# Linear attention in chunks: the product of queries and running states, as one product on 128 rows or as two on 64

## The chip, the cores and the metric

The kernel runs on one core of a Trainium2 chip. The core has five engines that work at the same time, each from its own queue in order: TensorE (PE, matrix products; its weight loads are shown as PEld), VectorE (DVE), ScalarE (ACT), GpSimd (POOL) and SyncE (SP), which here only starts transfers. The metric is the time on the device in microseconds (us), the median of several runs.

## The reference

Two transformer layers over 16 sequences (batches) of 512 tokens with 128 channels, all in float32. Each layer is: norm, scale and shift; an attention; a gated residual; norm, scale and shift; a feed-forward part; a gated residual.

In layer 0 the attention is causal and linear, with 16 heads of 8 channels. In layer 1 it is a retention with a decay per head, which has the same form once the decay is folded into q and k:

```python
# layer 0, for each token t and head:
S = S + kt[..., :, None] * vt[..., None, :]
z = z + kt
num = jnp.einsum('bhi,bhij->bhj', qt, S)
den = jnp.sum(qt * z, axis=-1, keepdims=True)
y = num / (den + EPS)
# layer 1:
retention = jnp.einsum('bhsd,bhtd->bhst', q, k) * SCALING * decay   # decay is 0 above the diagonal
out = jnp.einsum('bhst,bhtd->bhsd', retention, v)                    # then a norm per head and a gate
```

Layer 0's feed-forward part is a channel mix with a token shift. Layer 1's is an attention over the 16 batches at the same time step, followed by a choice of one of eight experts per token. This last part is called the routed half below.

## The kernel before

**Two halves.** The causal half runs both attentions and the channel mix, batch by batch (`both_layers`), and stores rows to DRAM (`token_rows`). The routed half reads them back by time step and runs the attention over batches and the experts. The change is in the causal half only.

**How a batch is laid out.** Channels lie on the 128 partitions (rows), tokens along the free dimension. The 16 heads are in four groups `r` of four (`RG`, `RH`); group `r` has the rows 32r to 32r+31 of q and k. The 512 tokens are 16 chunks of 32 (`NCH`, `CH`), in four blocks `g` of 128 tokens with four chunks `c` each; chunk number is `4 * g + c`. Each head has nine value columns, eight values and a one for the denominator (`HV`), so a group has 36 columns.

**The attention over chunks, `attended` (L659).** It has two parts that are planned side by side, and a third after both.

- `states_before`: the keys are turned (L672). PE forms, for each chunk, the products of keys and values (L685, tiles of 64 rows by 32 columns, 72 columns long). DVE masks away products of different heads (L699) and sums over chunks (a scan, L707). ACT and POOL each copy two of the four 32-row groups into `state` (L722). `state` is zero elsewhere, so it is a block diagonal: for each chunk 128 rows by 4 x 36 columns.
- `within_chunks`: ACT writes `kh`, the keys with one head each (L651). PE multiplies queries and keys inside each chunk on tiles of 32 rows by 32 columns (L752), two head groups at a time. ACT copies the scores (L761), PE turns them (L767), DVE applies the causal mask (L734). PE multiplies them with the values into two PSUM banks `o_ps` (L785), as tiles of 128 rows by 32 columns, 36 columns long.
- Last, PE adds queries times the state before the chunk (L801): one product per chunk from all 128 rows, 144 columns long, on a tile of 128 by 32. Bank `a` holds the blocks `g = 2a` and `2a + 1`. The first chunk has no state before it, so 15 products remain, in two bursts `n`.

Layer 0 divides the sums by the denominator (DVE, L870 to L872). Layer 1 takes a norm per head: ACT squares (L976), DVE sums (L978), ACT takes a root (L980), DVE divides (L982, L983). The result `y` is then turned and projected (L818, L602).

**The order of the work.** Each engine's order is written out by hand. Every chain of steps is a Python generator that yields marks such as `"P1.2"` (next comes a step on PE, planned at 1.2 us). `queued` keeps up to `WIDTH` = 5 batches running, always takes the step that can start first by its planned times, and emits its instructions; so the planned times and starts decide the order in every queue, including SP's, whose transfers wait in order as well. Batch n+1 may begin `SPACE` us of planned time after batch n, or when one of the five is done if that is later. Earlier batches have priority up to batch 12.

Of the kernel before, what the change touches and what calls it, by code (L numbers as in the profile page):

```python
# [22 lines left out]
F32 = mybir.dt.float32  # L23
# [6 lines left out]
P = 128  # L30
# [14 lines left out]
WIDTH = 5  # L45
CALM = 4.0
RUN, RUN_US = 5, 8.5
SPACE, SPACE2 = 10.0, 5.0
NX = WIDTH + 1
LATE = 12  # L50
LANDING = 4.5
# [161 lines left out]
def tile_adaln(ctx: ExitStack, tc: tile.TileContext, x, wa, wb, vec, wex, const, out):  # L213
# [122 lines left out]
    def groups(t):  # L336
        return t.rearrange("p (g m) -> p g m", m=P)
# [258 lines left out]
    def at_chunk(ch):  # L596
        return ch % NG * NC + ch // NG
# [61 lines left out]
    def attended(b, own_values, q, k):  # L659
# [57 lines left out]
        def copied(n, sums):  # L717
            yield "G1.5" if n else "A1.4"
            for r in range(n, RG, 2):
                rows = slice(r * 32, (r + 1) * 32)  # L720
                copy = nc.gpsimd.tensor_copy if n else nc.scalar.copy
                copy(state[rows, r], sums[rows])  # L722

        def within_chunks():
            yield "A2.7"

            kh = masked(own_set, k)
            by_block = q.rearrange("p (n s) -> p n s", s=CH)
            past = []

            def causal_only(rr, st_ps):
                yield "V1.3"
                for r, t in enumerate(st_ps):
                    tt(  # L734
                        sc[:, 2 * rr + r].rearrange("p (n t) -> p n t", t=CH),
                        t.rearrange("p (n t) -> p n t", t=CH),
                        causal.unsqueeze(1).to_broadcast([P, NCH, CH]),
                        ALU.mult,
                    )
                back(*st_ps)  # L740
                yield ""
                past.append(rr)

            for rr in range(2):
                s_ps = yield from banks(2)
                yield "P1.4"
                for n in range(NG):
                    for c in range(NC):
                        for r in range(2):
                            rows = slice((2 * rr + r) * 32, (2 * rr + r + 1) * 32)  # L750
                            at = at_chunk(n * NC + c)
                            mm(  # L752
                                groups(s_ps[r])[c * CH : (c + 1) * CH, n],
                                lhsT=by_block[rows, at],
                                rhs=kh[rows, at].rearrange("p m s -> p (m s)"),
                                start=True,
                                stop=True,
                            )
                yield "A1.2"
                for r in range(2):  # L760
                    nc.scalar.copy(sc[:, 2 * rr + r], s_ps[r])  # L761
                back(*s_ps)
                st_ps = yield from banks(2)
                yield "P1.25"
                for r in range(2):
                    for n in range(NG):
                        nc.tensor.transpose(  # L767
                            groups(st_ps[r])[:, n], groups(sc[:, 2 * rr + r])[:, n], ident
                        )
                yield Begun([causal_only(rr, st_ps)])  # L770

            yield ""
            while not past:
                yield "D0.1"
            yield from landed_at(("heads", own_values))
            o_ps.extend((yield from banks(2)))
            for r in range(RG):
                while len(past) <= r // 2:
                    yield "D0.1"
                yield "P0.45"  # L780
                for n in range(2):
                    for c, a in turns:
                        g = 2 * a + n
                        k0 = (n * RG + r) * RH * HV
                        mm(  # L785
                            o_ps[a][c * CH : (c + 1) * CH, k0 : k0 + RH * HV],
                            lhsT=groups(sc[:, r])[:, g, c * CH : (c + 1) * CH],
                            rhs=vh[:, g * NC + c, :, r * HV : (r + 1) * HV],
                            start=n == 0 and r == 0,
                            stop=False,  # L790
                            skip_group_check=True,
                        )

        turns = [(c, (c + d) % 2) for d in range(2) for c in range(NC)]
        yield [states_before(), within_chunks()]
        for n in range(2):
            yield "P1.2"
            for c, a in turns:
                ch = (2 * a + n) * NC + c
                if ch:  # L800
                    mm(  # L801
                        o_ps[a][c * CH : (c + 1) * CH, n * NH * HV : (n + 1) * NH * HV],
                        lhsT=q.rearrange("p (n s) -> p n s", s=CH)[:, at_chunk(ch)],
                        rhs=state[:, :, :, ch - 1].rearrange("p r j -> p (r j)"),
                        start=False,
                        stop=n == 1,
                        skip_group_check=True,
                    )
        free_values.append(own_values)
        free_sets.append(own_set)  # L810
        return o_ps, [o[:, 0 : 2 * NH * HV].rearrange("p (n k) -> p n k", k=HV) for o in o_ps]

    def closed(b, y, w, finish):

# [20 lines left out]
    def linear_attention(b):  # L835
        w = own(b, [P, NGATE, C], "gated")
        yield Begun([closing_weights(b, w)] + [next_entry(b + 1)] * (WIDTH <= b < B - 1))
        yield from landed_at(("x", b))
        h = work("h", b)
        yield from norm(b, mod0, 0, h, spread)  # L840
        own_values = yield from taken(free_values)
        qk = [work(tag, b) for tag in "qk"]

        def queries_and_keys():
            qk_ps = yield from banks(2)
            yield "P1.9"
            for a in range(2):
                mm(qk_ps[a], lhsT=wa_col(A_ATTN + a * C), rhs=h, start=True, stop=True)

            yield [positive(a, qk_ps[a]) for a in range(2)]  # L850

        def positive(a, ps):
            yield "A1.3"
            t = qk[a]
            nc.scalar.activation(t, ps, AF.Relu, scale=-1.0)
            nc.scalar.activation(t, t, AF.Exp, scale=-1.0)
            yield "V0.7"
            stt(t, ps, 0.0, t, ALU.max, ALU.add)  # L858
            back(ps)

        yield [
            queries_and_keys(),
            spread_values(b, h, wa_col(A_ATTN + 2 * C), own_values),
        ]
        o_ps, halves = yield from attended(b, own_values, *qk)
        y = work("q", b)
        for a, o in enumerate(halves):
            yield "V1.0"
            rd = own(b, [P, 2 * NH], "rd", bufs=2)
            ts(rd, o[:, :, HD], DEN_EPS, None, ALU.add)  # L870
            nc.vector.reciprocal(rd, rd)
            tt(  # L872
                y[:, a * 2 * C : (a + 1) * 2 * C].rearrange("p (n d) -> p n d", d=HD),
                o[:, :, 0:HD],
                rd.unsqueeze(2).to_broadcast([P, 2 * NH, HD]),
                ALU.mult,
            )
            back(o_ps[a])

        def finish(yt, y_ps):  # L880
            yield "A0.6"
            nc.scalar.copy(yt, y_ps)
            back(y_ps)

        yield from closed(b, y, w[:, 0], finish)
        return w
# [36 lines left out]
    def retention(b, w):  # L923
# [47 lines left out]

        def head_norm(a, o):
            yield "A0.4"
            yv = y[:, a * 2 * C : (a + 1) * 2 * C].rearrange("p (n d) -> p n d", d=HD)
            rd = own(b, [P, 2 * NH], "rd", bufs=2)
            nc.scalar.activation(yv, o[:, :, 0:HD], AF.Square)  # L976
# [6 lines left out]
            tt(yv, o[:, :, 0:HD], rd.unsqueeze(2).to_broadcast([P, 2 * NH, HD]), ALU.mult)  # L983
            back(o_ps[a])

        yield [head_norm(a, o) for a, o in enumerate(halves)]
# [830 lines left out]
```

## Time and profile before

| What | Value |
|---|---|
| Median of 3 runs | 1081.94 us (1080.48 to 1090.74) |
| The profiled execution | 1088.3 us, its span 1086.5 us |
| Mean granted TensorE clock | 0.923 |
| L801 in the causal half | 960 matmul instructions, 78.1 us busy |
| First and last of L801 | 56.4 and 700.6 us |
| Fetch of x by batch, from the sixth on (us) | 167.7, 195.8, 213.3, 251.4, 309.3, 376.0, 401.6, 430.3, 465.6, 519.1 |
| Last store of a residual (`token_rows<-k`) | 712.2 us |

A row of the profile names the line, the engine, the operation, the tile written and those read, their shapes, and how often. "128*32" ahead of a matmul's shape is the part of the 128 by 128 array that it uses. A float32 product appears as two matmul instructions. Busy time of a group is the union of its instructions, which on PE overlap. "Idle before" is the time in which the engine stood still just before instructions of the group, with what released them. The chain that ended last is followed back from the last instruction.

### The profile page before, as it was taken

Reading aid. Unit: us, or ns where it says so; the run is one execution under the profiler, and the core shown is the slowest. Engines: PE = TensorE matmul, PEld = TensorE weight load, DVE = VectorE, ACT = ScalarE, POOL = GpSimd, SP = SyncE. Lnnn points to the kernel's source line nnn. Section 1 sums busy time; section 2 is a strip of 40 time slices with the busy share of each in tenths; the row PEclk is TensorE's granted clock in tenths of the full one; section 3 lists DMA queues with packets and bytes.
Section 4 is the critical chain, followed back from the end, with each engine's and each line's share of the span. In section 5 each row is a group of like instructions: output and inputs, shape, how many; then the busy total and the mean of one; then the engine's idle time right before and its main releaser. Section 6 shows DMA issues by size and latency. Waiting matters only on the chain.

```text
span 1086.5 us, 37454 instructions
## 1 busy us (share of the span) xinstructions
PE 899.0 (83%) x15423; PEld 644.8 (59%) x15423; DVE 800.9 (74%) x2404; ACT 633.4 (58%) x1196; POOL 499.3 (46%) x621
## 2 busy tenths in 40 slices
PE   5798989896999898998889988738679777866985
PEld 4565666655666666665556665525456556755864
DVE  8567788885787889887688687647878767856444
ACT  3465554764645567574536555419878757744654
POOL 3313344542343453434343262234672565775676
PEclk9799999998899999999988998869788889998998
DMA  5624522524133333333232304050156364558763
GB/s 182 148 63 95 140 45 60 130 52 97 46 68 68 77 81 80 77 77 70 59 61 53 68 22 87 24 173 2 65 175 219 121 233 144 163 171 277 237 197 99
DMA packets 147851, 116.92 MB, mean 108 GB/s; under 512 B 75061, under 2 KB 127544, under 8 KB 147552
## 3 DMA queue, kind: packets, MB, share of 16 engines
q1 hardware_dynamic: 141024, 96.57, 33.9%
q0 software_dynamic: 6368, 17.08, 4.2%
q8 instruction: 122, 2.00, 0.7%
q10 hardware_dynamic: 288, 0.86, 0.3%
q14 instruction: 49, 0.40, 0.1%
HBM read 66.46 MB, written 39.04 MB: 97 GB/s over the span
## 4 chain that ended last, share of the span: by engine, by line
PE 41%; DVE 25%; ACT 10%; issue 8%; POOL 7%; DMA 6%; SPq 2%; POOLq 0%; another core or an unknown queue 0%; DVEq 0%; ACTq 0%
PE bank L602 6%; PE bank L801 4%; DVE q L550 4%; PE bank L752 3%; PE bank L767 3%; PE bank L1614 3%; PE bank L785 2%; PE bank L939 2%; PE bank L685 2%; DVE sc L734 2%; PE bank L940 2%; POOL out_x L1690 2%; DVE added L707 2%; DVE st L514 2%; DMA v_chunks<-values 2%
## 5 line engine op out<-in xcount | busy, mean ns | idle before, releaser
L761 ACT COPY sc<-bank 128x512 f32<-128x512 f32 x128 | 68.5, 588 | 78.9 <-PE bank L752 78.2
L550 DVE TENSOR_SCALAR q<-x,mv,rs 128x128 f32<-128x128 f32 x240 | 85.8, 421 | 21.6 <-POOL rs L523 13.9
L722 POOL COPY states<-added 32x576 f32<-32x576 f32 x64 | 43.5, 679 | 116.8 <-DVE added L707 91.2
L734 DVE TENSOR_TENSOR sc<-bank,con 128x512 f32<-128x512 f32 x128 | 81.8, 678 | 17.9 <-PE bank L767 12.9
L1690 POOL DMA_INDIRECT out_x<-z,l_to x71 | 71.4, 1005 | 41.4 <-ACT hid L1624 13.2
L752 PE MATMUL bank<-kh,q 32*32 32x128 f32 x4096 | 79.9, 279 | 8.3 <-DVE sc L734 2.6
L1614 PE MATMUL bank<-y,w 128*128 128x256 f32 (+1 forms) x312 | 78.5, 396 | 7.8 <-issue 4.6
L651 ACT ACTIVATE kh<-k,con 128x512 f32<-128x512 f32 x128 | 81.8, 715 | 1.9 <-DVE k L858 1.8
L801 PE MATMUL bank<-states,q 128*32 128x144 f32 x960 | 78.1, 424 | 4.4 <-issue 3.5
L1624 ACT ACTIVATE hid<-bank,w 128x256 f32<-128x256 f32 (+1 forms) x156 | 60.6, 464 | 27.6 <-PE bank L1614 12.3
L767 PE MATMUL bank<-ident,sc 128*128 128x128 f32 x512 | 72.4, 287 | 3.0 <-DVE q L858 1.4
L1441 POOL DMA_INDIRECT sorted_rows<-rows,idx x64 | 63.9, 998 | 21.7 <-issue 14.3
L752 PEld LDWEIGHTS bank<-kh,q 32*32 32x32 f32 x4096 | 59.9, 106 | 22.9 <-issue 6.4
L1634 PE MATMUL bank<-hid,w 128*128 128x256 f32 (+1 forms) x312 | 70.5, 372 | 3.1 <-ACT hid L1624 1.6
L1614 PEld LDWEIGHTS bank<-y,w 128*128 128x128 f32 x312 | 58.1, 207 | 20.9 <-issue 7.6
L523 POOL TENSOR_TENSOR rs<-rs,power 128x4 f32<-128x4 f32 x64 | 65.5, 1023 | 5.0
L566 ACT ACTIVATE h<-bank,mod 128x512 f32<-128x512 f32 x48 | 37.1, 777 | 52.2 <-PE bank L564 52.1
L767 PEld LDWEIGHTS bank<-ident,sc 128*128 128x128 f32 x512 | 59.6, 147 | 13.3 <-issue 7.2
L785 PEld LDWEIGHTS bank<-v_heads,sc 128*32 128x32 f32 x4096 | 49.3, 111 | 29.6 <-issue 16.1
L785 PE MATMUL bank<-v_heads,sc 128*32 128x36 f32 x4096 | 60.7, 202 | 6.3 <-issue 3.9
L685 PE MATMUL bank<-v_chunks,h 64*32 64x72 f32 x2048 | 49.7, 245 | 19.3 <-DMA v_chunks<-values 12.0
L522 POOL TENSOR_TENSOR rs<-mv,eps 128x4 f32<-128x4 f32 x64 | 14.4, 225 | 106.5 <-DVE mv L516 97.3
(276 smaller groups left out, 2300.8 us busy)
## 6 DMA issues: line engine op xcount, KB each, us to landing
w<-in_wex SPq DMA_DIRECT2D x39, 514.5 KB
x_in<-sorted_rows SPq DMA_DIRECT2D x32, 393.0 KB
v_rows<-values SPq DMA_DIRECT2D x32, 288.0 KB
v_chunks<-values SPq DMA_DIRECT2D x128, 72.0 KB
v_heads<-v_rows SPq DMA_DIRECT2D x128, 72.0 KB
rows<-token_rows SPq DMA_DIRECT2D x16, 512.0 KB
gated<-mod_rows SPq DMA_DIRECT2D x16, 384.0 KB
x<-in_x SPq DMA_DIRECT2D x16, 256.0 KB
```

Source lines behind the costliest of these rows:

```text
L550: ts(xn[:, g, :], X[b][:, g, :], mv[:, g, 0:1], rs[:, g : g + 1], ALU.subtract, ALU.mult,)
L651: nc.scalar.activation(t[:, :, n, :], k.rearrange("p (n s) -> p n s", s=CH), AF.Copy, scale=con[:, K_HEAD + n : K_HEAD + n + 1],)
L685: mm(d_ps[n][r * 32 : (r + 1) * 32, 0 : 2 * NG * RH * HV].rearrange("p (c g j) -> p c g j", c=2, g=NG)[:, :, g], lhsT=groups(kt)[rows, g, ...
L734: tt(sc[:, 2 * rr + r].rearrange("p (n t) -> p n t", t=CH), t.rearrange("p (n t) -> p n t", t=CH), causal.unsqueeze(1).to_broadcast([P, NC ...
L752: mm(groups(s_ps[r])[c * CH : (c + 1) * CH, n], lhsT=by_block[rows, at], rhs=kh[rows, at].rearrange("p m s -> p (m s)"), start=True, stop= ...
L761: nc.scalar.copy(sc[:, 2 * rr + r], s_ps[r])
L767: nc.tensor.transpose(groups(st_ps[r])[:, n], groups(sc[:, 2 * rr + r])[:, n], ident)
L785: mm(o_ps[a][c * CH : (c + 1) * CH, k0 : k0 + RH * HV], lhsT=groups(sc[:, r])[:, g, c * CH : (c + 1) * CH], rhs=vh[:, g * NC + c, :, r * H ...
L801: mm(o_ps[a][c * CH : (c + 1) * CH, n * NH * HV : (n + 1) * NH * HV], lhsT=q.rearrange("p (n s) -> p n s", s=CH)[:, at_chunk(ch)], rhs=sta ...
L1614: mm(h_ps[d][:, f % 2 * n : (f % 2 + 1) * n], lhsT=w[:, E_W1 + f * P : E_W1 + (f + 1) * P], rhs=y, start=True, stop=True,)
L1634: mm(o_ps[:, 0:n], lhsT=w[:, E_W2 + f * C : E_W2 + (f + 1) * C], rhs=hid[f // 2][:, f % 2 * n : (f % 2 + 1) * n], start=f == 0, stop=f == ...
L1690: sent = nc.gpsimd.indirect_dma_start(out=out_rows, out_offset=bass.IndirectOffsetOnAxis(ap=to[:, a : a + 1], axis=0), in_=z[:, a], in_off ...
```

## The change

The head groups are split in two halves `a`: groups 2a and 2a+1, which lie on the 64 rows from 64a on. Bank `a` of `o_ps` now holds the sums of half `a` of the heads for all four blocks, where it held all heads for two blocks. The product with the states becomes two products per chunk, each from 64 rows, 72 columns long. `state` keeps only 2 x 36 columns per chunk: group `r` is stored at `r % 2`. Within chunks, the two groups that are worked at a time are `rr` and `rr + 2`, one of each half, in place of `2 * rr` and `2 * rr + 1`. `y` is written through `half_of`, which picks half the heads in each of the four blocks. The planned times of the steps concerned change with them: a burst of products with the states from 1.2 to 0.75, zeroing a set of states from 2.0 to 1.1. `SPACE` goes from 10 to 12.

```diff
-SPACE, SPACE2 = 10.0, 5.0
+SPACE, SPACE2 = 12.0, 5.0
...
-        states.append(rp.tile([P, RG, RH * HV, NCH], F32, name=f"states{n}"))
+        states.append(rp.tile([P, 2, RH * HV, NCH], F32, name=f"states{n}"))
...
-            yield "G2.0"
+            yield "G1.1"
             nc.gpsimd.memset(states[n], 0.0)
...
-                copy(state[rows, r], sums[rows])
+                copy(state[rows, r % 2], sums[rows])
...
-                        sc[:, 2 * rr + r].rearrange("p (n t) -> p n t", t=CH),
+                        sc[:, rr + 2 * r].rearrange("p (n t) -> p n t", t=CH),
...
-                            rows = slice((2 * rr + r) * 32, (2 * rr + r + 1) * 32)
+                            rows = slice((rr + 2 * r) * 32, (rr + 2 * r + 1) * 32)
...
-            for r in range(RG):
-                while len(past) <= r // 2:
+            for rr in range(2):
+                while len(past) <= rr:
                     yield "D0.1"
-                yield "P0.45"
                 for n in range(2):
-                    for c, a in turns:
-                        g = 2 * a + n
-                        k0 = (n * RG + r) * RH * HV
-                        mm(
-                            o_ps[a][c * CH : (c + 1) * CH, k0 : k0 + RH * HV],
-                            lhsT=groups(sc[:, r])[:, g, c * CH : (c + 1) * CH],
-                            rhs=vh[:, g * NC + c, :, r * HV : (r + 1) * HV],
-                            start=n == 0 and r == 0,
+                    yield "P0.45"
+                    for g in (2 * n, 2 * n + 1):
+                        for c, a in turns:
+                            r = rr + 2 * a
+                            k0 = (2 * g + rr) * RH * HV
+                            mm(
+                                o_ps[a][c * CH : (c + 1) * CH, k0 : k0 + RH * HV],
+                                lhsT=groups(sc[:, r])[:, g, c * CH : (c + 1) * CH],
+                                rhs=vh[:, g * NC + c, :, r * HV : (r + 1) * HV],
+                                start=g == 0 and rr == 0,
...
         turns = [(c, (c + d) % 2) for d in range(2) for c in range(NC)]
         yield [states_before(), within_chunks()]
         for n in range(2):
-            yield "P1.2"
-            for c, a in turns:
-                ch = (2 * a + n) * NC + c
-                if ch:
-                    mm(
-                        o_ps[a][c * CH : (c + 1) * CH, n * NH * HV : (n + 1) * NH * HV],
-                        lhsT=q.rearrange("p (n s) -> p n s", s=CH)[:, at_chunk(ch)],
-                        rhs=state[:, :, :, ch - 1].rearrange("p r j -> p (r j)"),
+            yield "P0.75"
+            for g in (2 * n, 2 * n + 1):
+                for c, a in turns:
+                    ch = g * NC + c
+                    if ch:
+                        rows = slice(a * 64, (a + 1) * 64)
+                        mm(
+                            o_ps[a][c * CH : (c + 1) * CH, g * NH * HV // 2 : (g + 1) * NH * HV // 2],
+                            lhsT=q[rows].rearrange("p (n s) -> p n s", s=CH)[:, at_chunk(ch)],
+                            rhs=state[rows, :, :, ch - 1].rearrange("p r j -> p (r j)"),
...
+    def half_of(y, a):
+        return y.rearrange("p (g a n d) -> p a g n d", a=2, n=NH // 2, d=HD)[:, a]
...
-                y[:, a * 2 * C : (a + 1) * 2 * C].rearrange("p (n d) -> p n d", d=HD),
-                o[:, :, 0:HD],
-                rd.unsqueeze(2).to_broadcast([P, 2 * NH, HD]),
+                half_of(y, a),
+                o[:, :, :, 0:HD],
+                rd.unsqueeze(3).to_broadcast([P, NG, NH // 2, HD]),
...
-            yv = y[:, a * 2 * C : (a + 1) * 2 * C].rearrange("p (n d) -> p n d", d=HD)
+            yv = half_of(y, a)
```

More of the change, by code (lines that the diff above doesn't have):

```diff
@@ L760, in within_chunks @@
                 for r in range(2):
-                    nc.scalar.copy(sc[:, 2 * rr + r], s_ps[r])
+                    nc.scalar.copy(sc[:, rr + 2 * r], s_ps[r])
                 back(*s_ps)
@@ L767, in within_chunks @@
                         nc.tensor.transpose(
-                            groups(st_ps[r])[:, n], groups(sc[:, 2 * rr + r])[:, n], ident
+                            groups(st_ps[r])[:, n], groups(sc[:, rr + 2 * r])[:, n], ident
                         )
@@ L776, in within_chunks @@
             o_ps.extend((yield from banks(2)))
[L777 to L778 removed]
+            for rr in range(2):
+                while len(past) <= rr:
                     yield "D0.1"
[L780 removed]
                 for n in range(2):
[L782 to L792 removed]
+                    yield "P0.45"
[8 more added lines that the diff above has]
+                                start=g == 0 and rr == 0,
+                                stop=False,
+                                skip_group_check=True,
+                            )
         turns = [(c, (c + d) % 2) for d in range(2) for c in range(NC)]
@@ L796, in attended @@
         for n in range(2):
-            yield "P1.2"
-            for c, a in turns:
-                ch = (2 * a + n) * NC + c
-                if ch:
-                    mm(
-                        o_ps[a][c * CH : (c + 1) * CH, n * NH * HV : (n + 1) * NH * HV],
-                        lhsT=q.rearrange("p (n s) -> p n s", s=CH)[:, at_chunk(ch)],
-                        rhs=state[:, :, :, ch - 1].rearrange("p r j -> p (r j)"),
[L805 to L808, printed above, removed]
+            yield "P0.75"
[8 more added lines that the diff above has]
+                            rhs=state[rows, :, :, ch - 1].rearrange("p r j -> p (r j)"),
+                            start=False,
+                            stop=n == 1,
+                            skip_group_check=True,
+                        )
         free_values.append(own_values)
         free_sets.append(own_set)
-        return o_ps, [o[:, 0 : 2 * NH * HV].rearrange("p (n k) -> p n k", k=HV) for o in o_ps]
+        return o_ps, [
+            o[:, 0 : 2 * NH * HV].rearrange("p (g n k) -> p g n k", g=NG, k=HV) for o in o_ps
+        ]
+    def half_of(y, a):
+        return y.rearrange("p (g a n d) -> p a g n d", a=2, n=NH // 2, d=HD)[:, a]
     def closed(b, y, w, finish):
@@ L868, in linear_attention @@
             yield "V1.0"
-            rd = own(b, [P, 2 * NH], "rd", bufs=2)
-            ts(rd, o[:, :, HD], DEN_EPS, None, ALU.add)
+            rd = own(b, [P, NG, NH // 2], "rd", bufs=2)
+            ts(rd, o[:, :, :, HD], DEN_EPS, None, ALU.add)
             nc.vector.reciprocal(rd, rd)
             tt(
-                y[:, a * 2 * C : (a + 1) * 2 * C].rearrange("p (n d) -> p n d", d=HD),
-                o[:, :, 0:HD],
-                rd.unsqueeze(2).to_broadcast([P, 2 * NH, HD]),
+                half_of(y, a),
+                o[:, :, :, 0:HD],
+                rd.unsqueeze(3).to_broadcast([P, NG, NH // 2, HD]),
                 ALU.mult,
@@ L973, in head_norm @@
             yield "A0.4"
-            yv = y[:, a * 2 * C : (a + 1) * 2 * C].rearrange("p (n d) -> p n d", d=HD)
-            rd = own(b, [P, 2 * NH], "rd", bufs=2)
-            nc.scalar.activation(yv, o[:, :, 0:HD], AF.Square)
+            yv = half_of(y, a)
+            rd = own(b, [P, NG, NH // 2], "rd", bufs=2)
+            nc.scalar.activation(yv, o[:, :, :, 0:HD], AF.Square)
             yield "V0.4"
@@ L982, in head_norm @@
             nc.vector.reciprocal(rd, rd)
-            tt(yv, o[:, :, 0:HD], rd.unsqueeze(2).to_broadcast([P, 2 * NH, HD]), ALU.mult)
+            tt(yv, o[:, :, :, 0:HD], rd.unsqueeze(3).to_broadcast([P, NG, NH // 2, HD]), ALU.mult)
             back(o_ps[a])
```

## The prediction

> **What bounds the kernel now.** I read the engine table of the page first, then busy time by stretch, then the chain that ended last for the causal half alone, then the rows of the line that changes, then TensorE in order of time.
>
> ```profile
> PE 899.0 (83%) x15423; PEld 644.8 (59%) x15423; DVE 800.9 (74%) x2404; ACT 633.4 (58%) x1196; POOL 499.3 (46%) x621
> ```
>
> TensorE (PE) leads, but that is an average over two halves. By stretch (columns: us, busy of PE, PEld, DVE, ACT, POOL, clock, DMA share, GB/s):
>
> ```profile
> 0.00:54.00 54.00, 35.22 (x580) 25.97 (x588) 37.14 (x124) 23.71 (x39) 19.40 (x34) 0.87 0.62 165
> 54.00:650.00 596.00, 534.78 (x11683) 370.67 (x11669) 471.68 (x1242) 344.45 (x588) 240.34 (x273) 0.96 0.32 72
> 650.00:705.00 55.00, 45.25 (x974) 30.02 (x972) 40.20 (x99) 26.43 (x46) 14.99 (x17) 0.88 0.24 54
> 705.00:1086.50 381.50, 283.75 (x2202) 218.09 (x2202) 251.88 (x943) 238.80 (x524) 224.53 (x298) 0.88 0.49 162
> ```
>
> The causal half ends near 705 us. From 54 to 650 us PE is busy 89.7% and DVE 79.1%, so PE bounds this stretch with DVE close behind. The change touches nothing after 705 us. The chain from 54 to 650 us puts the changed line, L801, second:
>
> ```profile
> by line: PE bank L602 9.8%; PE bank L801 6.8%; issue 6.6%; DVE q L550 6.5%; PE bank L752 5.1%; PE bank L767 4.9%; PE bank L785 3.8%; DVE sc L734 3.3%; PE bank L939 3.3%; PE bank L685 2.7%; DVE added L707 2.7%; PE bank L940 2.6%; DVE st L514
> ```
>
> Over the whole span the same view gives L801 4.3%, 46.7 us. Its groups (busy us, mean ns of one; then idle before):
>
> ```profile
> L752 PE MATMUL bank<-kh,q 32*32 32x128 f32 x4096 | 79.9, 279 | 8.3 <-DVE sc L734 2.6
> ...
> L801 PE MATMUL bank<-states,q 128*32 128x144 f32 x960 | 78.1, 424 | 4.4 <-issue 3.5
> ...
> L685 PE MATMUL bank<-v_chunks,h 64*32 64x72 f32 x2048 | 49.7, 245 | 19.3 <-DMA v_chunks<-values 12.0
> ```
>
> So 46.7 of L801's 78.1 us, 60%, lie on the chain. "128*32" is the part of the array one instruction uses; four such parts side by side can work at once. L685 already has the shape that L801 would get, 64*32 with 72 columns, of which eight fit.
>
> **Part 1: two products on 64 rows.** The price comes from PE in order of time (start, duration, x instructions; every f32 product is two instructions):
>
> ```profile
> 304.70 0.36 PE L685 MATMUL bank<-v_chunks,h 64*32 64x72 f32 x16
> 304.99 1.19 PE L801 MATMUL bank<-states,q 128*32 128x144 f32 x14
> 306.11 0.39 PE L1036 MATMUL bank<-wgc,wvt 128*128 128x8 f32 x2
> ...
> 307.09 1.22 PE L801 MATMUL bank<-states,q 128*32 128x144 f32 x16
> 308.24 1.13 PE L903 MATMUL bank<-k,wa_sb 128*128 128x512 f32 x2
> ...
> 310.48 1.15 PE L752 MATMUL bank<-kh,q 32*32 32x128 f32 x64
> 311.56 0.70 PE L939 MATMUL bank<-h,wb_sb 128*128 128x512 f32 x1
> ...
> 698.80 2.19 PE L801 MATMUL bank<-states,q 128*32 128x144 f32 x30
> 700.92 2.07 PE L602 MATMUL bank<-gated,h 128*128 128x128 f32 x8
> ```
>
> From its start to the next line's start, a burst of 16 takes 1.15 us (307.09 to 308.24), that is four waves of four. The 30 at 698.80 are two bursts without anything between, eight waves, and take 2.12. Four more waves cost 0.97, so a wave is 0.243 us, and 0.18 per burst is a tail. A column of a wave is 0.243/144 = 1.69 ns. In L752 (eight waves of eight, 1.08 us) it is (1.08-0.18)/8/128 = 0.88 ns. L801 reads the states with a step of 16 values and L752 reads runs, so I take the factor of 1.9 as the price of the step. The step stays.
>
> After: a burst is 32 instructions in four waves of eight, 72 columns each: 4 x 72 x 1.69 = 0.487, plus 0.18 = 0.67 us. Saved 0.48 a burst, and 32 passes (16 batches, two layers) have two bursts each: 64 x 0.48 = 31 us of PE.
>
> Bounds for the wave, which no row of before shows in this form (half arrays that add into two banks). Above: the step costs nothing any more, 72 x 0.88, burst 0.43, 46 us saved. Below: only four parts work at once, eight waves of 0.122, burst 1.15, nothing saved. Worse, each wave keeping 0.243 and only four at once, would be 2.12 a burst; L685 speaks against it, since its 16 instructions on half arrays pass in 0.29 us. I take 31, because L685 shows eight at once in the same shape and the step is unchanged.
>
> A rule that speaks against it: the Trainium skill, "TensorE: Matmul & The Clock Gate", section on the 56 ns gap, has a floor of about 25 ns from one matmul's start to the next. By that 32 instructions need 0.80 us and the estimate would be 22 us saved. L685's 18 ns each (0.29/16) lie under that floor, so the row decides.
>
> What of the 31 is on the path? The chain holds 60% of L801, and 0.48 of 1.15 goes: 46.7 x 0.42 = 19.6 us. The other reading: between 54 and 650 us lie 596/644 of L801's bursts, 28.6 us of work; if PE stays at its 89.7%, the stretch falls from 596 to 506/0.897 = 564, 32 us. I take the chain, **-20**, since what is late next is DVE, at 79% already and 83% of a stretch shorter by 27.
>
> The 960 added matmuls and their weight loads lengthen PE's program. Idle time put down to "issue" just before PE's rows is 3.5 us at L801; doubled instructions may double it: +3.5 at most, zero at least. **+1**.
>
> **Part 2: the order of the heads.** The within-chunk blocks pair rows 0 with 2 and 1 with 3, where it was 0 with 1 and 2 with 3; L752, L761, L767, L734 and L785 keep count and shape. Zero. Bound: if 32-row parts of different halves could not run together, L752's eight waves become sixteen, +0.90 in each of 64 bursts, 58 us of PE. L685 runs the two 64-row halves together, which is why I take zero. Below nothing: pairs in different halves might run freer, at most L752's idle 8.3 us. L785 orders its bursts by the same two waits as before, two after each.
>
> Writing y (DVE L872, L983; ACT L976) becomes four blocks of 64 instead of one run of 256. Same count; L872's 424 ns stays. Bound: at L699's rate from PSUM (646 ns for 288) 574 ns, +0.15 x 64 = 10 us of DVE, which has 21% idle. Zero. The copies of the states (POOL 679 ns, ACT 666) keep their size.
>
> L801 now differs from L785 in form, where the two were alike. The second burst at 698.80 shows that a like neighbour saves the 0.18 tail: 64 x 0.18 x 60% = 7 us at worst. It becomes alike to L685, another frequent neighbour, so zero.
>
> **Part 3: zeroing half the states.** POOL's two memsets of 2.02 us near 3.6 us become about 1.0 each. POOL then idles 2.7 us until DVE's moments, which hides it: zero.
>
> **Part 4: chains 12 apart.** The planner starts the first five batches at 0, 12, 24, 36, 48 for 0, 10, 20, 30, 40. Later starts wait for a finished batch: x is fetched at 167.7, 195.8, 213.3 and so on, 17 us or more apart, so the spacing counts only at the start, where a DMA is last:
>
> ```profile
> 46.06 0.91 PE L685 MATMUL bank<-v_chunks,h 64*32 64x72 f32 x16 [3.27 <-DMA v_chunks<-values]
> ```
>
> SP's queue issues batch 3's weights (L582, 384 KB) at 37.2, just ahead of the v_chunks that PE waits for. With batch 3 planned 6 us later they may fall behind: -3.3 at best, that idle time. At worst batch 4, 8 us later, leaves all later 8 us later. PE is 91% busy from 54 to 81 us, so there is other work: **+1**.
>
> **The sum.** -20 + 1 + 1 = -18 us. The profiled execution took 1088.3 us (span 1086.5 and 1.8 around it), so 1070. It stood 6.4 above the median of the runs, 1081.94; the same 18 off the median gives **1064**.
>
> **The rivals.** (A) *DVE takes the place.* DVE is busy 83% and 86% from 300 to 400 and 400 to 500 us. If nothing is won there, and half of the chain's gain in the other 396 of 596 us: 20 x 0.66 x 0.5 = 6.6, less 2 of costs: -5, **1077**. For it: POOL and PE wait for DVE more than for any other engine. Against: PE leads DVE by ten points.
>
> (B) *The product gets no cheaper*, its half arrays taking turns: 0 + 2, **1084**. For it: no row adds into two banks from two halves at once. Against: L685 writes two so.
>
> (C) *Slower: the queues in their new order leave PE idle.* All queues are in order and the planner re-sorts them. Place: 54 to 650 us, PE waiting for DVE (L550, L675, L734). At the idle share of 200 to 300 us, 15.6%, the 506 us of work take 600, +4; at that of 650 to 705, 17.7%, 615, +19. Between, with the 2: +14, **1096**. It makes the kernel slower by over 1% from 16.4% idle on. For it: stretches of the same order differ from 6% to 18%. Against: PE's idle time before its rows is in many small pieces.
>
> (D) *The pairs 0/2 and 1/3 split L752's waves*: 58 x 60% less 18, +17, **1099**; it decides from bursts of about 1.6 us on.
>
> **How the numbers follow.** 1% is 10.8 us, about what a measurement of this kernel can tell from no change. Forecast 0.56 (its own range 1040 to 1071), A 0.20, B 0.06, C 0.14, D 0.04. Faster 0.56, same 0.26, slower 0.18. The range reaches from the PE reading with the startup gain and part of the free step (-32 - 3 - 4) to part of C, **1043 to 1092**; left out are most of C (0.09), D, and a larger gain (0.06), 0.19.
>
> **What would show it.** L801 as 64*32 64x72 x1920, busy near 47 us (78.1 now), bursts of 32 in 0.67; at 1.15, B. PE's busy total near 868. L752 at 80 us; more is D. The last residual row stored near 694 us (712.2 now). PE's idle share from 54 us to the end of the causal half below 12%; above 16% is C. L685's wait near 46 us shorter or gone if the start gains. What would make me wrong is mostly the order: 20 us are 3% of a half whose stretches differ by more.

## The result, and the profile after

The changed kernel took 1089.1 us (median of 12 runs, 1082.1 to 1098.3). The kernel before, on the same chip, took 1081.9 (12 runs). The ratio is 1.0055, with a 95% interval of 1.0029 to 1.0081: some 6 us slower, where 18 us faster was forecast. The profiled execution of after took 1083.75 us (span 1082.0), one of its faster ones; that of before, 1088.3, was one of before's slower ones. So the two spans by themselves say nothing of the sign, and the profile is read for where the time went.

The engine table of after, then its stretches (us, busy of PE, PEld, DVE, ACT, POOL, clock, DMA share, GB/s):

```profile
PE 877.5 (81%) x16383; PEld 649.5 (60%) x16383; DVE 802.5 (74%) x2404; ACT 633.6 (59%) x1196; POOL 506.6 (47%) x621
```

```profile
0.00:54.00 54.00, 37.62 (x653) 27.31 (x654) 37.70 (x114) 23.09 (x38) 14.90 (x31) 0.90 0.60 158
54.00:650.00 596.00, 519.18 (x12429) 377.52 (x12427) 471.07 (x1253) 347.97 (x590) 249.85 (x275) 0.93 0.32 73
650.00:705.00 55.00, 43.19 (x1128) 31.00 (x1110) 41.34 (x97) 24.23 (x45) 16.76 (x19) 0.81 0.25 54
```

The product's group, and a burst of it in order of time:

```profile
L752 PE MATMUL bank<-kh,q 32*32 32x128 f32 x4096 | 82.5, 287 | 10.6 <-DVE sc L734 3.8 <-issue 3.1 <-ACT kh L651 0.8
...
L804 PE MATMUL bank<-states,q 64*32 64x72 f32 x1920 | 50.1, 303 | 9.7 <-issue 8.6 <-POOL states L722 0.9
```

```profile
320.30 0.74 PE L804 MATMUL bank<-states,q 64*32 64x72 f32 x32
320.97 1.15 PE L752 MATMUL bank<-kh,q 32*32 32x128 f32 x64
```

The product itself did what was worked out. A burst of 32 takes 0.67 us (320.30 to 320.97), as forecast to the hundredth, and the row fell from 78.1 to 50.1 us. But from 54 to 650 us PE's busy time fell by only 15.6 us (534.78 to 519.18), its granted clock went from 0.96 to 0.93, and it stood idle for 77 us in place of 61. The last residual is stored at 709.9 us, 712.2 before. Three things need an explanation: why PE's other rows grew, what the new idle time waits for, and whether the new order costs anything. The chain that ended last can't help: in after it can be followed back only to the routed half.

### The profile page after: what moved, and what is told of

Its sections match the earlier page's. It is cut to its first block, busy times and chain, and to the rows that moved or that the text cites. A ratio compares the mean times of both kernels' runs of the same rounds, so it can differ in the third digit from the quotient of the medians.

```text
span 1082.0 us, 39341 instructions
## 1 busy us (share of the span) xinstructions
PE 877.5 (81%) x16383; PEld 649.5 (60%) x16383; DVE 802.5 (74%) x2404; ACT 633.6 (59%) x1196; POOL 506.6 (47%) x621
## 5 line engine op out<-in xcount | busy, mean ns | idle before, releaser
L550 DVE TENSOR_SCALAR q<-x,mv,rs 128x128 f32<-128x128 f32 x240 | 85.7, 422 | 17.5 <-POOL rs L523 12.5
L734 DVE TENSOR_TENSOR sc<-bank,con 128x512 f32<-128x512 f32 x128 | 81.8, 681 | 16.0 <-PE bank L767 15.8
L722 POOL COPY states<-added 32x576 f32<-32x576 f32 x64 | 46.2, 722 | 101.3 <-DVE added L707 86.6
L752 PE MATMUL bank<-kh,q 32*32 32x128 f32 x4096 | 82.5, 287 | 10.6 <-DVE sc L734 3.8
L1623 PE MATMUL bank<-y,w 128*128 128x256 f32 (+1 forms) x312 | 73.7, 380 | 6.4 <-ACT y L1613 3.6
L767 PE MATMUL bank<-ident,sc 128*128 128x128 f32 x512 | 75.3, 297 | 0.9 <-ACT sc L761 0.7
L752 PEld LDWEIGHTS bank<-kh,q 32*32 32x32 f32 x4096 | 61.9, 108 | 23.5 <-issue 8.6
L685 PE MATMUL bank<-v_chunks,h 64*32 64x72 f32 x2048 | 51.3, 250 | 25.9 <-DMA v_chunks<-values 14.2
L767 PEld LDWEIGHTS bank<-ident,sc 128*128 128x128 f32 x512 | 64.0, 154 | 9.6 <-issue 4.9
L786 PE MATMUL bank<-v_heads,sc 128*32 128x36 f32 x4096 | 60.3, 204 | 8.2 <-DVE sc L734 4.3
L1623 PEld LDWEIGHTS bank<-y,w 128*128 128x128 f32 x312 | 55.8, 199 | 18.0 <-ACT y L1613 7.0
L786 PEld LDWEIGHTS bank<-v_heads,sc 128*32 128x32 f32 x4096 | 47.5, 113 | 31.4 <-issue 17.6
L602 PE MATMUL bank<-gated,h 128*128 128x128 f32 x384 | 56.9, 295 | 9.1 <-DVE h L1002 4.9
```

Source lines behind the costliest of these rows:

```text
L550: ts(xn[:, g, :], X[b][:, g, :], mv[:, g, 0:1], rs[:, g : g + 1], ALU.subtract, ALU.mult,)
L734: tt(sc[:, rr + 2 * r].rearrange("p (n t) -> p n t", t=CH), t.rearrange("p (n t) -> p n t", t=CH), causal.unsqueeze(1).to_broadcast([P, NC ...
L752: mm(groups(s_ps[r])[c * CH : (c + 1) * CH, n], lhsT=by_block[rows, at], rhs=kh[rows, at].rearrange("p m s -> p (m s)"), start=True, stop= ...
L767: nc.tensor.transpose(groups(st_ps[r])[:, n], groups(sc[:, rr + 2 * r])[:, n], ident)
L786: mm(o_ps[a][c * CH : (c + 1) * CH, k0 : k0 + RH * HV], lhsT=groups(sc[:, r])[:, g, c * CH : (c + 1) * CH], rhs=vh[:, g * NC + c, :, r * H ...
L1623: mm(h_ps[d][:, f % 2 * n : (f % 2 + 1) * n], lhsT=w[:, E_W1 + f * P : E_W1 + (f + 1) * P], rhs=y, start=True, stop=True,)
```

## The experiments

Each is compared with the kernel before on the same chip, so the ratio is what counts; before took 1083, 1068, 1067 and 1086 us in the four groups of runs, and an expectation in us is to be read as a difference from the first of these. The clock is the mean granted TensorE clock over a kernel's runs, with that of before in the same group. "Row" is the busy time of the product with the states in the profiled execution.

| Kernel | Row, us | Matmul instructions of the row | Ratio to before, 95% | Clock (before) |
|---|---|---|---|---|
| before | 78.1 | 960 | 1 | 0.929 to 0.934 |
| after | 50.1 | 1920 | 1.0055 (1.0029 to 1.0081) | 0.908 |
| new product, old order | 48.6 | 1920 | 1.0023 (0.9993 to 1.0053) | 0.917 (0.930) |
| old product, new order | 76.5 | 960 | 1.0094 (1.0059 to 1.0129) | 0.921 (0.930) |
| new product, spacing 10 | 47.9 | 1920 | 1.0029 (0.9999 to 1.0059) | 0.919 (0.930) |
| old product split in two | 81.3 | 1920 | 1.0065 (1.0033 to 1.0096) | 0.930 (0.930) |
| half the columns | 45.9 | 960 | 0.9926 (0.9896 to 0.9957) | 0.924 (0.932) |
| new product, filler | 48.6 | 1920, filler 128 | 1.0096 (1.0067 to 1.0125) | 0.929 (0.932) |
| nearly no product | 25.8 | 128 | 0.9977 (0.9957 to 0.9998) | 0.895 (0.932) |
| half the mask | 78.1 | 960 | 0.9910 (0.9886 to 0.9933) | 0.934 (0.932) |
| states by chunk, old product | 49.3 | 960 | 1.0147 (1.0121 to 1.0173) | 0.918 (0.934) |
| states by chunk, new product | 36.0 | 1920 | 1.0230 (1.0203 to 1.0257) | 0.898 (0.934) |
| half the columns, filler | 44.3 | 960, filler 128 | 1.0061 (1.0031 to 1.0092) | 0.930 (0.934) |
| before, spacing 12 | 75.9 | 960 | 1.0044 (1.0024 to 1.0065) | 0.929 (0.934) |
| old product, filler | 76.0 | 960, filler 128 | 1.0178 (1.0156 to 1.0200) | 0.937 (0.929) |
| half the copies | 77.8 | 960 | 0.9914 (0.9883 to 0.9944) | 0.931 (0.929) |
| half copies, half columns | 45.8 | 960 | 0.9881 (0.9851 to 0.9910) | 0.919 (0.929) |

### Is it the order?

The planner's times decide the order, so product and order can be exchanged separately. With the planned times and the spacing of before, every engine runs the steps of before in the order of before:

```diff
-SPACE, SPACE2 = 12.0, 5.0
+SPACE, SPACE2 = 10.0, 5.0
-            yield "G1.1"
+            yield "G2.0"
-            yield "P0.75"
+            yield "P1.2"
```

> The changed kernel's two products on 64 rows, with the planned times and the spacing of before (1.2, 2.0, 10), so that every engine's order is that of before. Theory ORDER (the 28 us of TensorE are won, the new order and spacing lose them again): 1062 us, 20 below before, last residual stored near 694 us. Theory ABSORBED (TensorE's time is not what sets the end; waits for other engines, for instructions and a lower clock take the place): within 6 us of before, 1076 to 1088, TensorE's idle share from 54 to 650 us up from 10% to 13%, L804 busy 50 us against 78.

Measured 1.0023, +2.5 us (-0.8 to +5.7): not the 20 us below before that the order theory asked for. The product earns nothing even where no step changed its place.

The other corner, before's code with the three lines above turned round:

> The product of before on 128 rows in the changed kernel's order (planned 0.75 and 1.1, spacing 12). ORDER: 20 to 25 us above before, 1104, as the order costs what the product won. ABSORBED: the order costs little, 1082 to 1092, and the changed kernel is no faster than this one by more than 6 us.

Measured 1.0094, +10 us, just past the second expectation. So the new order does cost something, and the product wins 4 us of it back (1.0094 to 1.0055), if that much: the intervals of the two kernels overlap. Part of the cost shows in the waits of PE from 54 to 650 us (us in total, times, longest), here of the old product in the new order:

```profile
PE bank L685 <- DMA v_chunks<-values: 10.9, 4, 5.2
```

In after this line reads 10.6, in before 1.4: the values reach L685 later in the new order, whichever product is used. PE's idle time in all grew by less, from 61.2 to 65.9 us.

The spacing alone, with the new product and without it:

> The changed kernel with batches 10 apart in place of 12. If the spacing is what loses the gain: 1065. ORDER without a part for the spacing, or ABSORBED: 1080 to 1095, some 8 us from the changed kernel either way, as any other order.

> Before with batches 12 apart, nothing else. If the spacing holds most of the cost that the changed order showed with the old product (10 us): 8 to 12 us above before, with v_chunks waits and the fifth batch later. If it is any reordering of the queues: somewhere from 4 below to 10 above.

1.0029 for the new product with 10, against 1.0055 with 12, a difference inside the noise; 1.0044 for the old one with 12, and that wait stands at 6.3 us. With the old product, spacing 12 costs some 5 us by itself, about half of what the order costs. The first expectation (1065 or 1080 to 1095) fell on its second side; the second asked for 8 to 12, or for anything from -4 to +10, and 4.7 us is no clear vote. Order is a cost of this change, but not the place where 20 us went.

### Do the instructions cost?

Before, with each product on 128 rows split:

```diff
-                    mm(
-                        o_ps[a][c * CH : (c + 1) * CH, n * NH * HV : (n + 1) * NH * HV],
...
-                        rhs=state[:, :, :, ch - 1].rearrange("p r j -> p (r j)"),
+                    for part in range(2):
+                        k0 = (2 * n + part) * NH * HV // 2
+                        mm(
+                            o_ps[a][c * CH : (c + 1) * CH, k0 : k0 + NH * HV // 2],
...
+                            rhs=state[:, 2 * part : 2 * part + 2, :, ch - 1].rearrange("p r j -> p (r j)"),
```

> Before, each product on 128 rows split into two of 72 columns: the array's work as before (eight waves of 0.122 in a burst in place of four of 0.243), TensorE's instructions as many as in the changed kernel. Theory FETCH (more instructions make TensorE wait for them): +8 to +12 us, 1092, with the idle time put down to issue from 14 to 23 us. If instructions cost nothing: 1080 to 1084, issue as before.

Measured 1.0065, +7 us (3.6 to 10.4), a little under the +8 to +12 of theory FETCH, with the array's work unchanged (a burst of 32 still takes 1.15 us):

```profile
L803 PE MATMUL bank<-states,q 128*32 128x72 f32 x1920 | 81.3, 302 | 3.0 <-issue 2.6 <-ACT states L722 0.2
```

PE's idle time put down to issue between 54 and 650 us went from 12.2 to 17.5 us, and the row grew by 3.2. In the new product with the old order it is 21.3 us, and three of PE's five largest waits are of that kind:

```profile
PE bank L786 <- issue: 9.4, 7, 2.3
PE bank L564 <- DVE h L675: 6.0, 1, 6.0
PE bank L752 <- issue: 5.5, 4, 1.9
PE bank L564 <- DVE q L881: 5.0, 4, 2.6
PE bank L804 <- issue: 4.7, 4, 1.5
```

They fall on neighbours of the product as well (L786, L752). This idle time by itself is no measure of the instructions, though: half the columns, with no instruction added, has 16.6 us of it, and nearly no product, with only 128 matmuls left, has 12.0, of which 7.8 are still ahead of L786. The counterpart leaves out half the product instead of doubling it: the first 72 of the 144 columns, the history of half the heads.

> Before, with only the first 72 of the 144 columns of each product on 128 rows (the history of half the heads is left out): TensorE's array time for it halved as in the changed kernel, its instructions as few as before, every order as before. If the doubled instructions are what ate the gain: 1083 less 20, 1063. If they ate 7 us, as splitting cost, and the rest is eaten by a lower clock and waits: 1074 to 1080, mean granted clock 0.915 to 0.92 against 0.931.

Measured 0.9926, -8 us, as the second theory said; the clock 0.924, a little above it. The array time of the row is that of the new product (45.9 against 48.6 us), the instructions half. Between the two lie 0.0097, 10 us, for 960 matmuls and their loads, and for whatever else the new layout brings (the banks by half the heads, the pairs of groups, `y` in blocks): half the columns keeps the layout of before. So splitting alone shows 7 us for the instructions, and 10 is an upper figure with the layout in it. What remains of a saving of 32 us of PE, with nothing else changed, is 8 us and not 20.

### What takes the rest? The clock, as far as it can be counted

The same PE time, given back as useless work: one dense product per burst into columns of the bank that nothing reads.

```diff
+            mm(
+                o_ps[n][:, 2 * NH * HV :],
+                lhsT=ident,
+                rhs=q[:, 0 : T - 2 * NH * HV],
+                start=False,
+                stop=False,
+                skip_group_check=True,
+            )
```

> The new product in the old order, with one useless dense product (128 by 128, 224 columns, some 0.4 us) ahead of each of the 64 bursts: 26 us of TensorE's time given back for 128 more instructions. If TensorE's time sets the end: 20 us above the new product in the old order, 1105. If the freed time only came back as a lower clock and as idle time: the clock returns to 0.93 and the time stays within 6 us, 1084 to 1091.

> Half the columns of the old product (half the heads' history left out), with the useless dense product of 0.4 us ahead of each burst: array time of before, instructions of before plus 128. The same filler on the new product was 10 us above before. If the 960 added matmuls cost some 7 us by themselves: within 4 us of before, clock 0.93. If the filler's own time did it: 8 to 10 us above.

> Before, with the useless dense product (128 by 128, 224 columns) ahead of each of the 64 bursts: TensorE's time above that of before, the orders as before. Taking 32 us of TensorE away by half the columns won 8 us and cost 0.008 of clock. If the worth of TensorE's time is small both ways: +6 to +9 us. If it is the clock that makes taking away worth so little, adding must cost more than taking away wins: +14 to +20 us, clock 0.935 to 0.94.

The filler was dearer than planned, 0.55 us each (the last kernel, in order of time), 35 us in all:

```profile
314.11 0.62 PE L798 MATMUL bank<-q,ident 128*128 128x224 f32 x2
314.66 1.23 PE L809 MATMUL bank<-states,q 128*32 128x144 f32 x16
```

On the new product it cost 8 us (1.0023 to 1.0096) and the clock came back from 0.917 to 0.929: less than 20 and more than 6, between the two expectations. On half the columns it cost 14 us, so the kernel with the instructions and about the array time of before is 6.5 us above it, outside the 4 that were allowed; how far a product in a form of its own costs more than its length is not separated here. On before itself it cost 19 us, and the clock rose to 0.937. So 35 us of PE put in cost 19, and 32 taken away won 8.

Then nearly all of the product was left out, one per burst kept so that every wait stays:

```diff
-                    if ch:
+                    if ch and g == 2 * n + 1 and (c, a) == turns[-1]:
```

> The new product in the old order with one product per burst in place of 14 or 16 (nearly all history between chunks is left out; the waits stay): TensorE loses a further 40 us and 1792 of its 1920 added matmuls. If its time set the end: 1040. If clock and waits take most of it: one sixth of 68 us and the 7 us of instructions, 1064 to 1072, clock below 0.91.

Measured 0.9977, -2.5 us, well short of the 11 to 19 expected. The kernel with half the columns has 20 us more in the row and 832 more matmuls, and is 5 us *faster* (0.9926; the two intervals only meet, at 0.9957). What differs is the clock, 0.895 against 0.924, and the layout: nearly no product has that of after, half the columns that of before. No run takes the product out of the old layout, so the layout's share of the 5 us is not known. The stretch from 54 to 700 us of half the columns, then of nearly no product:

```profile
54.00:700.00 646.00, 559.50 (x12645) 399.97 (x12640) 508.55 (x1333) 370.25 (x631) 254.06 (x289) 0.92 0.31 71
```

```profile
54.00:700.00 646.00, 557.63 (x11817) 396.68 (x11805) 506.03 (x1330) 368.75 (x628) 253.78 (x289) 0.90 0.31 71
```

PE is busy the same 558 to 560 us, though the row is 20 us shorter. The others are longer by about that much, for example L752, whose bursts of 64 take 1.08 us at full rate in either layout:

```profile
L752 PE MATMUL bank<-kh,q 32*32 32x128 f32 x4096 | 81.3, 282 | 9.2 <-issue 3.2 <-DVE sc L734 2.9 <-ACT kh L651 1.6
```

```profile
L752 PE MATMUL bank<-kh,q 32*32 32x128 f32 x4096 | 85.6, 293 | 11.3 <-issue 4.2 <-DVE sc L734 3.7 <-ACT kh L651 0.9
```

How the clock falls can be seen in stretches of the new product in the old order:

```profile
92.20:95.60 3.40, 3.37 (x50) 2.35 (x33) 3.37 (x11) 1.23 (x3) 1.80 (x3) 1.00 0.33 86
95.60:99.00 3.40, 0.78 (x28) 0.64 (x32) 3.33 (x8) 2.87 (x6) 1.16 (x2) 1.00 0.82 201
99.00:102.40 3.40, 3.40 (x35) 1.68 (x22) 1.15 (x4) 1.68 (x3) 0.00 (x0) 0.51 0.39 117
...
167.30:170.70 3.40, 1.88 (x86) 1.22 (x76) 3.33 (x17) 0.00 (x0) 2.04 (x3) 1.00 0.35 95
170.70:177.50 6.80, 6.80 (x135) 4.95 (x126) 4.30 (x20) 4.21 (x8) 2.18 (x3) 0.50 0.32 93
```

A stretch of 3.4 us with PE busy 0.78 is followed by one at half the clock, in which PE is busy throughout; busy 1.88 of 3.40 is followed by two. Two bursts at half rate, of L752 in the last of these stretches and of the product later in the same kernel (granted clock 0.50 from 444 to 446 us), each with the line that follows:

```profile
170.89 1.95 PE L752 MATMUL bank<-kh,q 32*32 32x128 f32 x64
172.78 0.49 PE L685 MATMUL bank<-v_chunks,h 64*32 64x72 f32 x16
...
444.71 0.74 PE L804 MATMUL bank<-states,q 64*32 64x72 f32 x32
445.39 0.71 PE L786 MATMUL bank<-v_heads,sc 128*32 128x36 f32 x32
```

L752's burst takes 1.89 us in place of 1.08. The product's takes 0.68, as at full rate (0.67 to 0.73 in the three whole bursts of 32 found at half rate): with its step of 16 it does not lengthen. (Stored in runs, in two kernels below, it does lengthen: a burst of 32 from 0.41 to 0.66 us, one of 16 from 0.63 to 1.12.) So the change saves time in a row that the lower clock leaves alone, and the lower clock is paid by others.

Over the whole trace the changes of the clock lie on a fixed grid of 3.413 us. Of this kernel's full-rate intervals between 54 and 700 us, worked out from the clock records and the matmuls, those with PE busy under 50% were followed by half rate 7 times in 7, 50 to 60% 8 in 12, 60 to 80% 4 in 29, above 80% never in some 112. In before it is 5 in 5, 8 in 10, 2 in 21 and none in some 135. In the other fifteen kernels together it is less sharp: 113 in 129, 57 in 113, 37 in 372 and 6 in 1865. So whatever shortens PE's work pushes more intervals into the range where the clock drops, and each that falls costs up to 1.7 us of PE work (half of 3.413), less where PE idles or works at the product with the step. Half rate lasted 62 us between 54 and 700 us in before, 99 in the new product with the old order, 133 in nearly no product. In half the columns it lasted 99 as well, so in the profiled executions the clock took about the same from that kernel as from the new product, and by this count the 10 us between the two are not the clock's.

The Trainium skill, "TensorE: Matmul & The Clock Gate", Part 1, has the same free-running interval, 3413 ns, and two rates, and puts the fall to half rate after an idle interval. Here no whole interval of idling is needed: one with PE busy 50 to 60% of the time was followed by half rate in 8 cases of 12.

### Which engine or passage sets the end?

Before, with the causal mask on half of the scores, the rest unmasked:

```diff
-                        sc[:, 2 * rr + r].rearrange("p (n t) -> p n t", t=CH),
-                        t.rearrange("p (n t) -> p n t", t=CH),
-                        causal.unsqueeze(1).to_broadcast([P, NCH, CH]),
+                        sc[:, 2 * rr + r, 0 : T // 2].rearrange("p (n t) -> p n t", t=CH),
+                        t[:, 0 : T // 2].rearrange("p (n t) -> p n t", t=CH),
+                        causal.unsqueeze(1).to_broadcast([P, NCH // 2, CH]),
```

> Before, with the causal mask on half of the scores (the rest is left unmasked): VectorE loses 128 x 0.3 = 38 us, TensorE nothing. If VectorE's time and the waits for it set the end, it is worth more than TensorE's: 1055 to 1062. If TensorE's does: 1076 to 1083. If neither is free to shorten it alone: about a third, 1070.

```profile
L734 DVE TENSOR_TENSOR sc<-bank,con 128x256 f32<-128x256 f32 x128 | 48.6, 414 | 16.8 <-PE bank L767 10.7 <-issue 5.9
```

DVE lost 33 us (81.8 to 48.6); the time fell by 9.6 us, between the 13 expected for "neither" and the up to 7 for PE. DVE isn't the one bound either.

Before, with the states stored chunk by chunk, so that the product reads a run and the copies write with a step:

```diff
-        states.append(rp.tile([P, RG, RH * HV, NCH], F32, name=f"states{n}"))
+        states.append(rp.tile([P, NCH, RG, RH * HV], F32, name=f"states{n}"))
-                copy(state[rows, r], sums[rows])
+                copy(state[rows, :, r].rearrange("p c j -> p j c"), sums[rows])
-                        rhs=state[:, :, :, ch - 1].rearrange("p r j -> p (r j)"),
+                        rhs=state[:, ch - 1].rearrange("p r j -> p (r j)"),
```

> Before, every order as before, with the states stored chunk by chunk, so that a product on 128 rows reads 144 values in a run and the copies of the states write with a step. If the step is what costs 1.69 against 0.88 ns a column: bursts of 16 in 0.69 us in place of 1.15, L801 busy 48 us, and as with half the columns the time falls 4 to 10 us and the clock to 0.924; 1.5 us less for each 0.1 us that the 64 copies of ACT and POOL take longer. If the step costs nothing: bursts and time as before.

> The new product in the old order, with the states stored chunk by chunk as well. Bursts of 32 in 0.43 to 0.45 us; TensorE 46 us less than before. If the clock and the instructions take it back: no faster than the stored-by-chunk product on 128 rows, within 5 us of before, clock 0.90 to 0.91. If TensorE's time counts: 12 us under before.

The first of the two in order of time, and its copies:

```profile
308.39 0.70 PE L801 MATMUL bank<-states,q 128*32 128x144 f32 x16
309.02 1.13 PE L903 MATMUL bank<-k,wa_sb 128*128 128x512 f32 x2
```

```profile
L722 POOL COPY states<-added 32x576 f32<-32x576 f32 x64 | 77.2, 1207 | 116.7 <-DVE added L707 110.3 <-PE bank L602 4.7
L722 ACT COPY states<-added 32x576 f32<-32x576 f32 x64 | 75.5, 1180 | 29.1 <-DVE added L707 28.6
```

A burst falls from 1.15 to 0.63 us, so the step of 16 was indeed what made a column dear. But each copy went from 666 and 679 ns to 1180 and 1207, and the kernel is 16 us slower, not the 4 to 10 faster less some 8 that was expected. Against half the columns, which has the same PE time and the short copies, it is 24 us slower (1.0147 to 0.9926). ACT and POOL are 61% and 44% busy in this kernel from 54 to 650 us, so they are not full. On each of the two engines two copies stand one after the other between the sum over chunks and its products, in each of 32 passes: 2 x 0.52 x 32 = 33 us of added delay, of which 24 arrive at the end. With the new product as well it is 25 us above before, where at most 5 were expected; the row fell to 36.0 us, the clock to 0.898.

So the copies' passage was shortened, one copy per engine in place of two (the history of head groups 2 and 3 is left out), and then together with half the columns:

```diff
-            for r in range(n, RG, 2):
+            for r in range(n, 2, 2):
```

> Before, with one copy of the states each on ScalarE and GpSimd in place of two (the history of head groups 2 and 3 is left out): 21 us less on each of two engines that are not full, 0.67 us less between the sum over chunks and its products in each of 32 passes; TensorE as before. If the wait from sum to product is what the end hangs on, as when the copies became longer: 15 us faster (0.7 us for each of 21), clock 0.93. If TensorE or VectorE is full and sets the end: within 4 us of before.

> Half the copies and half the columns of the product (same half of the history left out). If the copies' wait hid the worth of TensorE's time: more than the sum of the two alone, over 23 us faster. If the clock is what takes TensorE's time back: no more than their sum, 15 to 20 us faster, clock 0.915 to 0.92.

0.9914, -9 us, where 15 or next to nothing was expected: the passage counts, though less in this direction than in the other. Both together gave 0.9881, -13 us, less than the sum of the two alone (8 + 9) and than the 15 to 20 expected, at a clock of 0.919. A shorter passage does not make PE's time worth more.

## Why the prediction was wrong

**The mechanism and its size were right.** The bursts (0.67 us), eight half arrays at a time, the price of the step (0.63 us a burst without it, where the factor of 1.9 would make it 0.69) and 28 of the 31 us of PE all came out. Rival B (no cheaper) falls. Rival D falls: L752's bursts still take 1.08 us with the pairs 0/2 and 1/3, and its row grew only with the clock. Zero for y stands as far as its rows go: writing it takes 425 and 424 ns on DVE and 382 on ACT, as before (425, 424 and 380). For the zeroing no run shows a cost.

**The step that failed is "what of the 31 is on the path": -20.** It took the share of the chain and left everything else at its length. PE saved alone, with no instruction added and no order changed, is worth 8 us (half the columns). The step supposed that PE's rows don't depend on how full PE is, and the sum has no term for the clock. They do depend on it: the freed time makes emptier intervals, and many of these are followed by half rate, 99 us of it in place of 62. From before to the new product in the old order, between 54 and 700 us, the row lost 29.5 us and PE's busy time 14.6 (576.63 to 562.03): half of the saving came back as longer matmuls (the 37 us more of half rate account for up to 18). The other half came back as idle time, 9 us of it put down to issue and the rest mostly to DVE. The chain of before named what came last, not what would come last next.

**The term for the instructions, +1, was mis-sized**: splitting alone measured +7; the comparison at equal array time, +10, has the layout in it. The row that it was taken from, issue before L801, left out the neighbours: with the product split, the wait before the row itself fell from 3.5 to 2.6 us and that before L785 rose from 3.9 to 8.4.

**The term for the spacing and the order, +1, was mis-sized**: the order costs 10 us with the old product, spacing 12 alone about 5, with the new product the two together 3.5 (1.0023 to 1.0055, within the noise). The hoped-for gain near 46 us did appear: PE's wait for DMA before 54 us is 3.6 us in after, 6.9 before. It was lost again later, in the waits for v_chunks.

Put together: -8 for PE's time, +10 for instructions and layout, +3.5 for the order, some +6. These are the steps from before over half the columns and the new product in the old order to after, so they must add up to what was measured; the two terms that were measured by themselves on the old product, +7 and +10, would give +9 with the same -8. Rival C named the order, and needed 16% idle; PE's idle share from 54 to 650 us is 12.9%. Rival A had the place of the gain taken by DVE alone: its gain of 6.6 from PE is near the 8 of half the columns, but its end, 5 below before, is 11 from the measured one, and DVE was at most a part of the cause.

**What stays open.** No run here holds the clock while PE's work shrinks, so the clock's share of the end is argued from accounting and from one pair (nearly no product against half the columns), not isolated, and that pair differs in layout too; that adding PE time costs more than removing wins fits the clock, but also a PE that is simply fuller. What the new layout costs with the product as it was is not tested. Of what the wait "issue" consists the profile does not say. Differences of 3 us between two kernels are at the edge of what these runs tell. None of the kernels with the whole computation beat before.

## What to carry to other kernels

A saving on TensorE need not be worth its share of the chain: look at the granted clock by stretches of a few microseconds, count how many lie near the busy share at which it drops, and expect a good part of a saving back as longer matmuls elsewhere. A product cut into twice the instructions can pay for them even if the array does half the work, so compare at equal instruction counts, and in the same layout, before counting on a tile rate. Where several engines are 60 to 90% busy, test the short serial passages between them (a copy, a scan) first: here 33 us more there cost 24 and 21 us less won 9, while on the busiest engine 35 us more cost 19 and 32 less won 8.

## What the runs showed that was not expected

- The clock falls after a single interval of 3.413 us that is only partly idle. In all seventeen kernels together, below 50% busy it fell after 125 of 141 intervals, between 50 and 60% after 73 of 135, above 80% after 6 of some 2100.
- At half rate the product with its step of 16 does not lengthen (0.68 us a burst), while L752, which reads runs, goes from 1.08 to 1.89.
- Less work, later end: 20 us and 832 matmuls fewer, 5 us slower, with the clock at 0.895 in place of 0.924 (and in the other layout).
- A copy of 32x576 float32 inside SBUF that writes with a step of 144 values takes 1180 ns on ScalarE and 1207 on GpSimd, against 666 and 679 in runs. Reading with a step of 16 makes a burst of the product 1.15 us long, against 0.63 in runs.
- Matmul and weight load of a narrow tile are not free: 960 more pairs at equal array work cost 7 us (3.6 to 10.4), some 7 ns each.
